# Attention weights exponentiated into transposed squares and turned by VectorE, with their sums from a column of ones, in a two-layer graph kernel

## Chip, cores and metric

One core of one Trainium2 chip. The metric is device time in microseconds of one execution; the median of three runs of the kernel before is 3092.37 us (3086.59 to 3094.2). Profiled executions have a span of their own (3078.1 us here), on which the shares of the profile are taken.

## The reference, cut to what matters

128 graphs of 64 nodes with 768 features pass two layers. Everything is float32.

```
# layer 0
p = softmax(h h^T / sqrt(768)) * adj;  attn = p / sum(p)
ctx = triu(attn,1) (h Wl^T + bl) + diag(attn) (h Ws^T + bs) + tril(attn,-1) (h Wr^T + br)
x = layernorm(h + relu(layernorm(ctx) * gamma + beta))
# layer 1, 12 heads of 64
q, k, v = x Wq + bq, x Wk + bk, x Wv + bv
scores = where(adj > 0, q k^T / 8 + beta * adj, -9e15)
out = layernorm(x + softmax(scores) v)
```

The softmax of layer 1 is what the change is about: the weighted sum of values can be divided by the sum of the exponentials afterwards.

## The kernel before, in words

The 8192 rows are walked in 16 blocks of 512 tokens (8 graphs; T = 4 tiles of 128 rows, each with two graphs). Each large product is computed by a seven-product (Strassen-Winograd) scheme, `seven()`: 7 products in the order 1, 2, 6, 5, 7, 4, 3, each in two halves j, so 14 *places* of six matmuls each. `by_tokens()` uses it for the self, left, right and value weights (128x384 a matmul), `projected()` for queries and keys (128x256), one call for each of three head groups of four heads. The two accumulators are ps_X (products 1, 6, 7, 4) and ps_Y (2, then 5 and 3), each one PSUM bank for each j. ScalarE evicts ps_X in `projected` (L522, L528) and VectorE adds it to ps_Y (L530); in `by_tokens` VectorE does both (L298 and the lines L392, L410, L501). A bank that still accumulates has to be read before its next product starts: product 7 is read while one place passes, before product 4; the other reads have three places.

A block n passes these parts in order: left (`side_part(m, "l")`, m = n + 1), right, self (`self_part`), val (`values(n)`), then `projected` three times. Layer 0 of block m and layer 1 of block n overlap, and the attention of block n - 1's last head groups is done inside the left part of block n. From the first block on, the program's order is kept as written. Two things set it: *hooks*, a table that says at which place of which part a step stands ahead of the products, and two *queues*, urgent and lazy. After each place `step()` issues one item of the queues, urgent ones first; an item marked "act" (ScalarE) or "gap" lets a lazy one follow in the same step, and no "act" item is issued after the second half of product 5 or the first half of product 7. `settle(key)` issues at once whatever is left of a key.

For a head group, `scores()` computes q k^T in 64x64 products, four in the array at a time (L548), scales and masks (L552, L567), subtracts the maximum (L568, L569), exponentiates (L570), sums (L563), divides (L564, L571). `turned_weights()` transposes the result on TensorE against an identity (L586), eight transposes for each head group, copied out of PSUM by ScalarE (L587). `weighted()` multiplies with the values (L600), and two queue items add the outcome to the residual (L606). The values of both graphs of a tile are kept so that the row half of the array matches the head's parity: `values()` evicts each result in four pieces of 64 rows (L501). `finish()` normalises and stores.

PSUM: two banks each for ps_X and ps_Y, two for transposes (ps_tr, tag tr), two for everything else (ps_mm). Weights stream from DRAM on SyncE's queue through four buffers (L293, L516); `loads()` fetches x for the residual (L728) there too, at places 0 to 3 of the self part; `squares()` loads a block in 32x32 squares on ScalarE's queue (L202), for layer 1 from place 9 of the right part, and `turned()` transposes the squares on VectorE (L211) in the self part from place 3.

Of the kernel before, what the change touches and what calls it, by code (L numbers as in the profile page):

```python
# [11 lines left out]
F32 = mybir.dt.float32  # L12
AF = mybir.ActivationFunctionType
# [31 lines left out]
def gnn_two_layers(ctx: ExitStack, tc, x, adj, wl, bl, ws, bs, wr, br, gamma, beta,  # L45
# [11 lines left out]
    wst = ctx.enter_context(tc.tile_pool(name="wst", bufs=4))  # L57
    st = ctx.enter_context(tc.tile_pool(name="st", bufs=2))
    ps_st = ctx.enter_context(tc.tile_pool(name="ps_st", bufs=2, space=PSUM))
    ps_tr = ctx.enter_context(tc.tile_pool(name="ps_tr", bufs=2, space=PSUM))  # L60
    ps_mm = ctx.enter_context(tc.tile_pool(name="ps_mm", bufs=2, space=PSUM))

    x_t = x.rearrange("b l d -> (b l) d").rearrange("(n t p) d -> n t p d", t=T, p=P)
    x_b = x.rearrange("b l d -> (b l) d").rearrange("(n k) d -> n k d", k=NTOK)
# [46 lines left out]
    def act(f):  # L111
        return f, "act"
# [17 lines left out]
    def settle(key):  # L130

        for queue in (urgent, lazy):
            while any(item[0] == key for item in queue):
                queue.popleft()[1]()


# [50 lines left out]
    def transposed(src, xT, t):  # L187

        for c0 in range(0, KC, 3):
            ps = ps_tr.tile([P, 4, P], F32, tag="tr", name="ps_x")  # L190
            for c in range(3):
                nc.tensor.transpose(ps[:, c, :], src[:, c0 + c :: KC], ident)
            nc.scalar.copy(xT[:, c0 : c0 + 3, t * P : (t + 1) * P], ps[:, 0:3, :])
# [179 lines left out]
    def sides(n):  # L373

        blk = blocks[n]
        settle(("a", n))
        aps = ps_tr.tile([P, T, P], F32, tag="tr", name="ps_a")
        for t in range(T):
            nc.tensor.transpose(aps[:, t, :], blk["a2"][:, t].rearrange("p c m -> p (c m)"), ident)  # L379
        aT = l0.tile([P, T, P], F32, tag="aT", name=f"aT_{n}")  # L380
        nc.vector.tensor_tensor(aT, aps, side.rearrange("p g l -> p (g l)")[:, None, :].to_broadcast([P, T, P]),
                                ALU.mult)
        blk["aT"] = aT
# [99 lines left out]

        return one, two

    def values(n, hooks={}):


        blk = blocks[n]
        v = l1_p.tile([P, T, 2, HP, HD], F32, tag="v", name=f"v_{n}")  # L490
        blk["v"] = v

        def last(t, h, ps, part):
            def pairs(a):
                return a.rearrange("p (j r d) -> p r j d", r=2, d=HD)

            add = pairs(bias["v"][:, h * HALF : (h + 1) * HALF] if part is None else part)
            for r in range(2):
                for g in range(2):
                    rows = slice(g * L, (g + 1) * L)  # L500
                    nc.vector.tensor_tensor(v[r * L : (r + 1) * L, t, g, h * 3 : (h + 1) * 3, :],  # L501
                                            pairs(ps)[rows, r], add[rows, r], ALU.add)

        by_tokens("v", blk["S"], last, None, hooks)

    def projected(n, hg, hooks={}):

# [24 lines left out]
        seven(HTOK, factors, first, last, hooks, True)  # L532
        blk["qk"] = qk

    def scores(n, hg, pool=None):

        blk = blocks[n]
        q, k = blk["qk"]

        s = (pool or l1s_p).tile([P, T, 2, 2, L], F32, tag="lr" if pool else "s", name="s")  # L540
        sc = [ps_mm.tile([P, T, 2, L], F32, tag="mm", name=f"sc{r}") for r in range(2)]
        for t in range(T):
            for c in range(2):
                for r in range(2):
                    rows = slice(r * HD, (r + 1) * HD)
                    for g in range(2):
                        tok = slice(t * P + g * L, t * P + (g + 1) * L)
                        nc.tensor.matmul(sc[r][g * L : (g + 1) * L, t, c, :], lhsT=q[rows, c, tok],  # L548
                                         rhs=k[rows, c, tok], start=True, stop=True)
        m8, add = blk["m8"], blk["add"]  # L550
        for r in range(2):
            nc.vector.tensor_tensor(s[:, :, :, r, :], sc[r], m8[:, :, None, :].to_broadcast([P, T, 2, L]), ALU.mult)  # L552
        s4 = s.rearrange("p t c r m -> p t (c r) m")
        s8 = s.rearrange("p t c r m -> p (t c r) m")
        mx = st.tile([P, T * 4], F32, tag="mx1", name="mx1")
        z = st.tile([P, T * 4], F32, tag="z1", name="z1")
        rz = st.tile([P, T * 4], F32, tag="rz1", name="rz1")

        def per_row(v):
            return v[:, :, None].to_broadcast([P, T * 4, L])  # L560

        def sums():
            nc.vector.tensor_reduce(z, s8, AX.X, ALU.add)  # L563
            nc.vector.reciprocal(rz, z)  # L564

        later(("s", n, hg),
              lambda: nc.vector.tensor_tensor(s4, s4, add[:, :, None, :].to_broadcast([P, T, 4, L]), ALU.add),  # L567
              lambda: nc.vector.tensor_reduce(mx, s8, AX.X, ALU.max),  # L568
              lambda: nc.vector.tensor_tensor(s8, s8, per_row(mx), ALU.subtract),  # L569
              act(lambda: nc.scalar.activation(s8, s8, AF.Exp)), GAP, sums,  # L570
              lambda: nc.vector.tensor_tensor(s8, s8, per_row(rz), ALU.mult), queue=urgent)  # L571
        blk[hg] = s

    def turned_weights(n, hg, tiles=range(T), pool=None):

        blk = blocks[n]
        settle(("s", n, hg))
        e = blk[hg]
        if 0 in tiles:
            blk["eT", hg] = (pool or l1_p).tile([P, T, 2, P], F32, tag="lr" if pool else "eT", name="eT")  # L580
        eT = blk["eT", hg]
        for t0 in tiles[::2]:
            ps = ps_tr.tile([P, 4, P], F32, tag="tr", name="ps_e")
            for t in range(2):
                for c in range(2):
                    nc.tensor.transpose(ps[:, 2 * t + c, :], e[:, t0 + t, c].rearrange("p r m -> p (r m)"), ident)  # L586
            nc.scalar.copy(eT[:, t0 : t0 + 2].rearrange("p t c i -> p (t c) i"), ps)  # L587

    def weighted(n, hg, tiles=range(T)):

        blk = blocks[n]
        xt, v, eT = blk["x"], blk["v"], blk["eT", hg]
        y = [ps_mm.tile([P, T, 2, HD], F32, tag="mm", name=f"ps_y{r}") for r in range(2)]
        for t in tiles:
            for c in range(2):
                for r in range(2):
                    rows = slice(r * L, (r + 1) * L)
                    for g in range(2):
                        cols = slice(g * L, (g + 1) * L)
                        nc.tensor.matmul(y[r][cols, t, c, :], lhsT=eT[rows, t, c, cols],  # L600
                                         rhs=v[rows, t, g, hg + c * HC, :], start=True, stop=True)

        def added(t):
            res = xt[t].rearrange("p (c k r d) -> p r c k d", c=2, k=HC, r=2)
            for r in range(2):
                nc.vector.tensor_add(res[:, r, :, hg, :], res[:, r, :, hg, :], y[r][:, t])  # L606

        def both(ts):
            for t in ts:
                added(t)  # L610

        later(("y", n, hg), *[partial(both, tiles[i : i + 2]) for i in range(0, len(tiles), 2)], queue=urgent)

    def finish(n, tiles=range(T)):
        xt = blocks[n]["x"]
# [60 lines left out]
    blocks[0]["S"] = combined(blocks[0]["xT"])  # L676
    start.close()
    l1_p = ctx.enter_context(tc.tile_pool(name="l1", bufs=1))
    l1s_p = ctx.enter_context(tc.tile_pool(name="l1s", bufs=2))

# [3 lines left out]
    for n in range(NBLK):  # L686
# [12 lines left out]
        last = n == NBLK - 1  # L699
        if p >= 0:  # L700
            one, two, three = (left, left, right) if not last else (qk[0], qk[1], qk[1])
            at(one, 1 if not last else 2, scores, p, 2)
            at(one, 1 if not last else 2, turned_weights, p, 1)
            at(one, 5, weighted, p, 1)
            at(two, 11 if not last else 2, turned_weights, p, 2)
            at(two, 13 if not last else 5, weighted, p, 2)
            at(three, 0 if not last else 6, finish, p)

        if not last:
            if n > 0:  # L710
# [6 lines left out]
                    settle(("o", n))  # L717
                    blocks[n]["sq1"], sq1["fs"] = squares(blocks[n]["x_d"])

                at(right, 9, begin1)  # L720
                fetch = {}

                def begin2():
                    fetch["fs"] = loads(m)

                at(own, 0, begin2)
                for t in range(T):
                    at(own, t, lambda t=t: fetch["fs"][t]())  # L728
                for a in range(P // Q):
                    at(right, 9 + a, lambda a=a: sq1["fs"][a]())  # L730
                at(own, 0, settle, ("f", p))

                def turn1():
# [43 lines left out]
        at(qk[1], 2, scores, n, 0)  # L777
        at(qk[2], 2, scores, n, 1)
        if not last:
            at(qk[2], 2, turned_weights, n, 0)  # L780
            at(qk[2], 5, weighted, n, 0)
        for hg in range(NHG):
            projected(n, hg, qk[hg])
    n = NBLK - 1
    values(n, {2: [partial(scores, n, 2, l0t)]})

    for t0 in (0, 2):
        for hg in range(NHG):
            turned_weights(n, hg, range(t0, t0 + 2), l0t if hg else None)
        for hg in range(NHG):  # L790
            weighted(n, hg, range(t0, t0 + 2))
            settle(("y", n, hg))
        finish(n, range(t0, t0 + 2))
        settle(("f", n))


# [29 lines left out]
```

## Time and profile before

| | before |
|---|---|
| median of runs | 3092.37 us |
| span of the profile | 3078.1 us |
| TensorE clock granted | 0.992 |
| TensorE busy / VectorE / ScalarE / GpSimd | 97% / 72% / 13% / 12% |
| TensorE busy from 200 to 2800 us | 2550.7 of 2600 us |
| one block in the middle | about 188 us |
| DMA moved | 541.2 MB, 176 GB/s over the span |

A row of groups gives the line, engine and operation, output and inputs with their shapes and count, then busy time in us and mean ns of one instruction, then the idle time of that engine before these instructions and what ended it. Matmuls are pipelined: the mean of one includes time in which the one before still runs, so the busy time, not count times mean, is what the group takes of the engine. A row of waits names who waited for whom, the total in us, how often, and the longest.

### The profile page before, as it was taken

The numbers are of one execution on the slowest core, as the hardware profiler recorded it, in microseconds if no ns is written. First come the engines' busy times: TensorE is split into PE (matmuls) and PEld (weight loads), VectorE is DVE, ScalarE is ACT, GpSimd is POOL, SyncE is SP. The second block draws the span as 40 slices with busy tenths as digits, with TensorE's granted clock in tenths as the row PEclk, the third lists the DMA queues.
The fourth block names the chain that finished last, engine by engine and source line by source line (L and its number), as shares of the span: only waits on it lengthen the run. The fifth ranks groups of instructions, "written<-read, shape, count | busy, mean of one in ns | idle before, by whom it ended". The sixth has DMA issues, their size and how long they took to land.

```text
span 3078.1 us, 45049 instructions
## 1 busy us (share of the span) xinstructions
PE 2983.9 (97%) x18144; PEld 2015.0 (65%) x18144; DVE 2227.8 (72%) x4163; ACT 396.8 (13%) x691; POOL 354.3 (12%) x317
## 2 busy tenths in 40 slices
PE   8899999999999999999999999999999999999997
PEld 5457657576675766758567585665757667575685
DVE  5758767686776867768687686867768677686756
ACT  0101102021020200202011020110201102020031
POOL 2321010110101101011010111101011010110000
PEclk9999999999999999999999999999999999999998
DMA  8663655737557474574645756456573655746433
GB/s 284 211 230 121 190 174 166 216 118 217 152 161 213 124 229 139 161 215 145 212 139 162 211 160 208 132 179 191 161 221 119 215 156 162 220 127 220 128 123 119
DMA packets 261070, 541.20 MB, mean 176 GB/s; under 512 B 28576, under 2 KB 165408, under 8 KB 260864
## 3 DMA queue, kind: packets, MB, share of 16 engines
q1 hardware_dynamic: 185424, 429.38, 44.1%
q10 hardware_dynamic: 60848, 44.05, 7.2%
q0 software_dynamic: 14592, 64.89, 5.4%
q8 instruction: 145, 2.38, 0.3%
q14 instruction: 61, 0.50, 0.0%
HBM read 473.37 MB, written 64.88 MB: 175 GB/s over the span
## 4 chain that ended last, share of the span: by engine, by line
PE 77%; DVE 7%; issue 7%; DMA 7%; POOL 1%; ACT 0%; ACTq 0%; SPq 0%; POOLq 0%; DVEq 0%
PE ps_X L269 38%; PE ps_Y L269 30%; DMA ws<-in_L_gnn_W_self_dram 6%; DVE v L501 4%; PE ps_ctx L425 3%; DVE hT L211 2%; PE sc L548 1%; PE ps_y L600 1%; PE u L331 1%; PE ps_e L586 1%; DVE u L298 1%; DMA b_l<-in_L_gnn_W_left_dram 1%; DVE stats L239 0%; PE ps_a L379 0%; DMA d_v<-t_v 0%
## 5 line engine op out<-in xcount | busy, mean ns | idle before, releaser
L269 PE MATMUL ps_X<-xT,wqk 128*128 128x256 f32 x1728 | 388.8, 379 | 0.0
L269 PEld LDWEIGHTS ps_X<-xT,wqk 128*128 128x128 f32 x1728 | 328.2, 190 | 48.1 <-issue 0.4
L269 PE MATMUL ps_Y<-S,wqk 128*128 128x256 f32 x1152 | 264.3, 379 | 0.0
L410 DVE TENSOR_TENSOR lr<-ps_Y,u 64x384 f32<-64x384 f32 x384 | 213.2, 555 | 62.6 <-PE ps_Y L269 56.2
L522 ACT ACTIVATE uqk<-ps_X,bq 128x256 f32<-128x256 f32 x144 | 68.2, 474 | 1419.5 <-PE ps_X L269 1419.5
L269 PEld LDWEIGHTS ps_Y<-S,wqk 128*128 128x128 f32 x1152 | 218.9, 190 | 29.8
L269 PE MATMUL ps_X<-wv,xT 128*128 128x384 f32 x576 | 199.2, 492 | 0.3
L239 DVE BATCH_NORM_STATS2 stats<-o 128x6 f32<-128x384 f32 x384 | 192.4, 542 | 1.8
L269 PE MATMUL ps_X<-ws,hT 128*128 128x384 f32 x540 | 181.7, 491 | 7.4 <-DMA ws<-d_s 7.4
L269 PE MATMUL ps_X<-wl,hT 128*128 128x384 f32 x540 | 183.7, 486 | 0.0
L269 PE MATMUL ps_X<-wr,hT 128*128 128x384 f32 x540 | 179.1, 486 | 0.0
L501 DVE TENSOR_TENSOR v<-ps_Y,u 64x192 f32<-64x192 f32 x384 | 136.4, 355 | 41.7 <-PE ps_Y L269 35.6
L269 PE MATMUL ps_Y<-xT,wqk 128*128 128x256 f32 x576 | 138.7, 386 | 27.8 <-DVE v L501 17.9
L269 PEld LDWEIGHTS ps_X<-wv,xT 128*128 128x128 f32 x576 | 106.7, 190 | 85.8 <-issue 9.6
L269 PEld LDWEIGHTS ps_X<-ws,hT 128*128 128x128 f32 x540 | 103.5, 192 | 79.8 <-issue 9.7
L269 PEld LDWEIGHTS ps_X<-wr,hT 128*128 128x128 f32 x540 | 102.5, 190 | 71.3
L269 PEld LDWEIGHTS ps_X<-wl,hT 128*128 128x128 f32 x540 | 100.4, 190 | 61.1
L269 PE MATMUL ps_X<-S,wqk 128*128 128x256 f32 x576 | 138.2, 385 | 0.0
L269 PEld LDWEIGHTS ps_Y<-xT,wqk 128*128 128x128 f32 x576 | 104.3, 190 | 51.6 <-issue 23.8
L298 DVE TENSOR_TENSOR u<-ps_X,bv 128x384 f32<-128x384 f32 x96 | 53.5, 557 | 114.7 <-PE ps_X L269 114.1
L298 DVE TENSOR_TENSOR u<-ps_X,bl 128x384 f32<-128x384 f32 x96 | 53.4, 556 | 112.5 <-PE ps_X L269 110.6
L619 POOL DMA_DIRECT2D out_dram<-o x64 | 34.6, 541 | 862.2 <-DVE o L618 862.0
(183 smaller groups left out, 4715.2 us busy)
## 6 DMA issues: line engine op xcount, KB each, us to landing
wqk<-qk_d SPq DMA_DIRECT2D x336, 384.0 KB, 3.0
wv<-d_v SPq DMA_DIRECT2D x64, 576.0 KB, 4.8
ws<-d_s SPq DMA_DIRECT2D x60, 576.0 KB, 9.0
wl<-d_l SPq DMA_DIRECT2D x60, 576.0 KB, 5.0
wr<-d_r SPq DMA_DIRECT2D x60, 576.0 KB, 3.7
wv<-in_L_gnn_Wv_dram SPq DMA_DIRECT2D x48, 576.0 KB, 4.0
ws<-in_L_gnn_W_self_dram SPq DMA_DIRECT2D x45, 576.0 KB, 7.4
wl<-in_L_gnn_W_left_dram SPq DMA_DIRECT2D x45, 576.0 KB, 4.1
```

The costliest lines, as they stand in the source:

```text
L211: nc.vector.transpose(xT[:, c, :].rearrange("p (s j) -> p s j", j=Q), sq[:, :, c::KC])
L239: nc.vector.bn_stats(stats[:, h, :], tiles[t][:, h * HALF : (h + 1) * HALF])
L269: nc.tensor.matmul(ps, lhsT=a, rhs=b, start=(c == 0 and i in (1, 2, 5)), stop=(c == len(fs) - 1), skip_group_check=True)
L298: nc.vector.tensor_tensor(u, ps, bias[nm][:, b * HALF : (b + 1) * HALF], ALU.add)
L331: nc.tensor.matmul(u[g * L : (g + 1) * L, t, :], lhsT=xT[:, c, tok], rhs=xT[:, c, tok], start=(c == 0), stop=(c == KC - 1))
L410: nc.vector.tensor_tensor(lr[t][half * L : (half + 1) * L, g, cols], ps[rows], bias[nm][rows, cols] if part is None else part[rows], ALU.add)
L425: nc.tensor.matmul(ps[g * L : (g + 1) * L, 0:HALF], lhsT=blk["aT"][:, t, g * L : (g + 1) * L], rhs=blk["lr"][t][:, g, cols], start=True, s ...
L501: nc.vector.tensor_tensor(v[r * L : (r + 1) * L, t, g, h * 3 : (h + 1) * 3, :], pairs(ps)[rows, r], add[rows, r], ALU.add)
L522: nc.scalar.activation(u, ps, AF.Identity, bias=bias["qk"[j]][:, c : c + 1])
L548: nc.tensor.matmul(sc[r][g * L : (g + 1) * L, t, c, :], lhsT=q[rows, c, tok], rhs=k[rows, c, tok], start=True, stop=True)
L586: nc.tensor.transpose(ps[:, 2 * t + c, :], e[:, t0 + t, c].rearrange("p r m -> p (r m)"), ident)
L619: nc.gpsimd.dma_start(out=out_t[n, t], in_=xt[t])
```

## The change

The weights are no longer summed, divided and transposed by TensorE. The exponentials are written in 32x32 squares to where each square of the transpose stands (16 instructions of 32 partitions by 256 columns for a head group, issued in four groups, or two in the left part and for the last head group), and VectorE turns the squares in place (two transposes of 128x512). The values get a 65th column of ones for each head, so that the product with the weights has the sum of exponentials beside the 64 outputs; `added()` takes its reciprocal and multiplies and adds in one instruction for each tile and head. Values are evicted whole (one piece), and three ScalarE copies, queued after the value part, swap the halves that belong to the other rows; the last block evicts in place as before. The pool for transposes is gone and its two banks go to ps_mm (four). In `scores()`, any unfinished exponentials are settled first, as there is one score buffer instead of two, with two buffers for the transposed weights. The layer-1 squares are loaded from place 10 of the left part, and x from place 8 of the right part. In the left part the last head group's weighted sums stay ahead of place 13; its two turns are issued after places 11 and 12.

The diff, cut to its core:

```diff
-    ps_tr = ctx.enter_context(tc.tile_pool(name="ps_tr", bufs=2, space=PSUM))
-    ps_mm = ctx.enter_context(tc.tile_pool(name="ps_mm", bufs=2, space=PSUM))
+    ps_mm = ctx.enter_context(tc.tile_pool(name="ps_mm", bufs=4, space=PSUM))
...
+            if not in_place:
+                nc.vector.tensor_tensor(v[:, t, :, heads, 0:HD], pairs(ps), add, ALU.add)
+                return
...
+        if not in_place:
+            low, high = v[0:L, :, 1, :, 0:HD], v[L:P, :, 0, :, 0:HD]
+            swap = l0t.tile([P, T, HP, HD], F32, tag="lr", name="swap")
+            later(("v", n), act(lambda: nc.scalar.copy(swap[0:L], high)), act(lambda: nc.scalar.copy(high, low)),
+                  act(lambda: nc.scalar.copy(low, swap[0:L])), queue=urgent)
...
+        settle("e")
+        settle(("m", n))
...
-        def sums():
-            nc.vector.tensor_reduce(z, s8, AX.X, ALU.add)
-            nc.vector.reciprocal(rz, z)
...
+            for a in groups:
+                rows = slice(a * Q, (a + 1) * Q)
+                for b in range(P // Q):
+                    cols = slice(b * Q, (b + 1) * Q)
+                    nc.scalar.activation(e[cols, :, rows], pairs[rows, :, cols], AF.Exp)
+
+        def turn(h):
+            e = blk["eT", hg][:, h * 2 : h * 2 + 2].rearrange("p t c i -> p (t c i)")
+            nc.vector.transpose(e, e)
...
-              act(lambda: nc.scalar.activation(s8, s8, AF.Exp)), GAP, sums,
-              lambda: nc.vector.tensor_tensor(s8, s8, per_row(rz), ALU.mult), queue=urgent)
+              *[act(partial(exponentials, range(a, a + at_once))) for a in range(0, P // Q, at_once)], GAP,
+              partial(turn, 0), partial(turn, 1), queue=urgent)
...
-        for t0 in tiles[::2]:
-            ps = ps_tr.tile([P, 4, P], F32, tag="tr", name="ps_e")
-            for t in range(2):
-                for c in range(2):
-                    nc.tensor.transpose(ps[:, 2 * t + c, :], e[:, t0 + t, c].rearrange("p r m -> p (r m)"), ident)
-            nc.scalar.copy(eT[:, t0 : t0 + 2].rearrange("p t c i -> p (t c) i"), ps)
...
+        def added(h, r):
+            ps = y[r, h]
+            rz = st.tile([P, 2, 2], F32, tag="rz1", name="rz1")
+            nc.vector.reciprocal(rz, ps[:, :, :, HD])
...
+                    nc.vector.scalar_tensor_tensor(res[:, r, c, hg, :], ps[:, t, c, 0:HD], rz[:, t, c : c + 1],
+                                                   res[:, r, c, hg, :], ALU.mult, ALU.add)
+
+
+        urgent.extendleft(reversed([(("y", n, hg), partial(added, h, r)) for h in halves for r in range(2)]))
...
-    l1s_p = ctx.enter_context(tc.tile_pool(name="l1s", bufs=2))
+    l1s_p = ctx.enter_context(tc.tile_pool(name="l1s", bufs=1))
+    l1e_p = ctx.enter_context(tc.tile_pool(name="l1e", bufs=2))
+
+    v = l1_p.tile([P, T, 2, HP, HD + 1], F32, tag="v", name="v")
+    nc.gpsimd.memset(v[:, :, :, :, HD], 1.0)
...
-            at(one, 1 if not last else 2, turned_weights, p, 1)
...
-            at(two, 11 if not last else 2, turned_weights, p, 2)
             at(two, 13 if not last else 5, weighted, p, 2)
...
-                at(right, 9, begin1)
+                at(left, 10, begin1)
...
-                at(own, 0, begin2)
+                at(right, 8, begin2)
```

## The prediction

> **What bounds the kernel now.** I read the page's busy table first, then the slices, the groups by line, TensorE's waits, and a timeline of one block.
>
> ```profile
> PE 2983.9 (97%) x18144; PEld 2015.0 (65%) x18144; DVE 2227.8 (72%) x4163; ACT 396.8 (13%) x691; POOL 354.3 (12%) x317
> ```
>
> The groups by line (busy us, mean ns of one, idle before):
>
> ```profile
> L269 PE MATMUL ps_X<-xT,wqk 128*128 128x256 f32 x1728 | 388.8, 379 | 0.0
> ...
> L501 DVE TENSOR_TENSOR v<-ps_Y,u 64x192 f32<-64x192 f32 x384 | 136.4, 355 | 41.7 <-PE ps_Y L269 35.6
> ...
> L586 PE MATMUL ps_e<-ident,s 128*128 128x128 f32 x384 | 53.1, 282 | 2.5 <-ACT eT L587 2.5
> ```
>
> TensorE is busy 97% of 3078.1 us at a granted clock of 0.992, and its matmuls carry the chain that ended last. So the change is worth what it takes from TensorE's own work and from its waits, less the waits it adds; VectorE (72%) and ScalarE (13%) have room on average, but in-order queues can be late in one place. The question is then where the 94 us lie in which TensorE is idle. Its waits (total, times, longest):
>
> ```profile
> PE ps_Y L269 <- DMA ws<-in_L_gnn_W_self_dram: 21.3, 13, 3.8
> PE ps_Y L269 <- DVE v L501: 17.9, 14, 1.3
> PE ps_Y L269 <- PE ps_X L269: 9.8, 14, 0.7
> ...
> PE ps_a L379 <- ACT eT L587: 4.1, 14, 0.3
> ```
>
> From 200 to 2800 us the stretches show 2550.7 us of TensorE in 2600: 49.3 idle. These four rows hold about all of it (one 3.8 us piece of the first lies earlier). The second and third are one event: the timeline shows the third ending 0.1 us after a value eviction (L501) does, so both are the first products of the query/key projection waiting for a PSUM bank whose values VectorE writes out in four pieces each. The first row is the self weights, late in each block while activations, squares and outputs are being moved (DMA share above 1 from 1320 to 1340 us).
>
> **What the Trainium skill says.** "ScalarE: Activation LUTs", section What ACT_TABLE_LOAD costs: an ACTIVATE with immediate scale and bias takes 186 ns + 0.833 ns an element, whatever the function. For 256 elements 399 ns; this trace has 417 (L350, 128x256), and I use 417. "VectorE: DVE Perf Modes", The three transpose paths: VectorE's transpose turns 32x32 blocks only, which is why the exponentials are written square by square; the trace shows L211 on such squares, 1091 ns for 128x512. "TensorE: Matmul & The Clock Gate", Step-by-step: what each phase is for: matmuls stay in program order, only weight loads are pulled ahead. So a matmul that waits holds all products behind it; no trace line here contradicts it.
>
> **The change part by part.**
>
> *Transposes.* 384 transposes of the weights leave TensorE: 53.1 us (L586). All lie on the path, so −53.1. The waits of the transpose behind ScalarE's copies (ps_a, 14 times 0.3) go with them: −4.1.
>
> *Exponentials.* 48 of 128x1024 (1057 ns) become 768 of 32x256. None of 32 partitions is in the trace; bounds: 417 ns (L350, same length) as the upper, about 310 if consecutive ones overlap as the skill's page says. I take 417: 16 x 0.417 = 6.7 us a head group, on ScalarE, which also evicts the projections. ScalarE's total: 396.8 − 50.7 − 51.3 (copies L587) + 768 x 0.417 + swaps 64 = 679 us, 22%. Queued behind a group of four exponentials (1.7 us) are the evictions of ps_X (474 ns), for which VectorE's add and TensorE's next product into that bank wait. A place of the projection is 1.3 us of TensorE (5.34 us for four). The tight bank is the seventh product's: it must be read within one place. The queue keeps exponentials out of the two places before it. In the block at 1420 the scores are ready (L569) at 1425.8; two groups then end at 1429.2, and the eviction there starts at 1429.25 and is due by 1430.4. The other evictions have three places, 4 us. So nothing on the path, with about 0.7 us to spare.
>
> *Turns.* 96 transposes of 128x512 on VectorE, 1.08 us each: 104 us. They replace the sums, their reciprocals and the scaling (58.3 + 12.1 + 58.5). Values whole: 512 pieces of 355 ns (181.9 us) become 120 of 557 and 32 of 355 (78 us). The weighted sums: 384 adds (82.5) become 768 of 64 columns and 192 reciprocals; between 162 ns (L360, 128x4) and 279 (L606, 128x128) I take 200: 154 + 35 us. VectorE: −393 + 371, about 2206 us (2175 to 2270). Its total hides under TensorE.
>
> *Values.* With one 0.56 us eviction instead of 1.46 us of four, VectorE has no backlog when the projection begins: −17.9 − 9.8 = −27.7. The three half-swaps are 15 x 3 copies of 64x1536, by the slope between 128x384 (478) and 128x512 (585) 1.43 us each, at the front of the first projection. They end some 30 us before the values are used (third projection), and delay evictions with four places of room: no cost.
>
> *Loads moved.* The squares go from the right part to the left part, x from the self part to the right part, so the two 1.5 MB sets no longer meet in the stretch with DMA share above 1. The stretches at the end of the left part have 0.3 to 0.5. The self weights then land in time: −17.5 (21.3 without the early piece of 3.8).
>
> *Ones column.* 3072 products of 65 columns for 64: 58.5/64 = +0.9.
>
> *The wait it adds.* In the left part the last head group's two turns are issued after places 11 and 12, and its weighted sums stand ahead of place 13. The timeline of one block, before:
>
> ```profile
> 1483.58 2.10 PE L269 MATMUL ps_X<-wl,hT 128*128 128x384 f32 x6
> ...
> 1485.52 2.10 PE L269 MATMUL ps_Y<-wl,S 128*128 128x384 f32 x6
> ...
> 1485.72 1.12 DVE L410 TENSOR_TENSOR lr<-ps_X,bl 64x384 f32<-64x384 f32 x2 [0.74 <-PE ps_X L269]
> 1487.55 1.16 PE L600 MATMUL ps_y<-v,eT 64*64 64x64 f32 x64
> 1487.65 1.12 DVE L410 TENSOR_TENSOR lr<-ps_Y,u 64x384 f32<-64x384 f32 x2 [0.81 <-PE ps_Y L269]
> 1488.64 2.20 PE L269 MATMUL ps_Y<-wl,S 128*128 128x384 f32 x6
> ```
>
> Put the turns in: eviction of place 11 to 1486.84, first turn to 1487.93; eviction of place 12 to 1489.05, second turn to 1490.14. The first half of the weighted products (0.55 us) can start at 1488.0, the second at 1490.2, and place 13 at 1490.75 instead of 1488.64: 2.1 us. Behind the waiting matmul is all of the right part, so it is on the path: 14 blocks x 2.1 = +29.4 (1.0 to 2.5 each: 14 to 35). The other two weighted sums have four or more places between turn and use.
>
> *Tail.* Before, 27.9 us pass from the last product (3050.20) to the end. After it VectorE has a turn more to do (1.1), six weighted sums of 2 reciprocals and 8 products (2.0 us instead of about 1.7 with the waits), but the last transposes and copies (2.2 us of wait) are gone and two head groups fit in the banks. I get 24.4 + 6.4 us of output DMA, about +3.
>
> Sum: −53.1 − 4.1 − 27.7 − 17.5 + 0.9 + 29.4 + 3 = −69. From 3092.4: **3023 us**.
>
> **Rivals.**
> 1. *The turns are no wait* (VectorE runs ahead, or the first half's products cover it): −98, 2994 us. For it: VectorE is idle 0.7 to 0.8 us before both evictions shown. Against: 2.2 us of work per 1.94 us place cannot be done before its inputs exist.
> 2. *ScalarE and the DMA take half back.* The loads now meet outputs and right weights, and the wait moves rather than goes (+17.5); an exponential of 0.55 us makes the two groups 4.4 us and the bank of the seventh product some 0.4 us late in 15 projections (+6); the turns cost the high 2.5 us each (+6): 3053 us. For it: only 0.7 us spare there, and x and outputs are still 3 MB together. Against: landing times of 3.7 to 5 us outside the crowded stretch, where a piece is issued some 12 us ahead.
> 3. *ScalarE becomes the bound of the projections*: small exponentials of 0.8 us would make 12.8 us for a head group against 5.2 us of products in its four places, leaving some 3 us uncovered after the evictions' slack in 2 projections of 15 blocks: +90 on my sum, 3113 us, slower. For it: 32-partition shapes are not in the trace, and the count rises from 48 to 768. Against: the price per element and the 128x256 row agree.
>
> **How the numbers follow.** My case 0.62, the first rival 0.13, the second 0.19, the third 0.06. The likeliest gives 3023. The low bounds of the turns (14 us) and a tail of 0 give 3005, the first rival 2994, the second 3053; the range takes in all of these, 2993 to 3054. Outside it are the third rival and the far sides of the first two, together under 2 in 10. Faster by over 0.3% (below 3083) holds in all but the third and odd cases: 0.92; same 0.02; slower 0.06.
>
> **What would show it.** No L586 or L587 groups; the waits on L501 and on the self weights gone from TensorE's list; instead a wait of ps_y on VectorE's transpose, 14 times, 1.5 to 2 us, in the left part. Exponentials near 417 ns, turns near 1.08 us, y products near 200. TensorE busy near 2932 us. It would be wrong if TensorE shows new waits on ScalarE's uqk, if a wait on wr or ws weights comes back, or if y products take over 300 ns.

## The result, and the profile after

The changed kernel takes 2997.33 us (2995.84 to 2998.13, four runs) against 3089.48 us of the kernel before measured beside it (3083.96 to 3094.2, four runs): a ratio of 0.9702 [0.9683, 0.9721], or −92 us. The prediction was 3023 us, −69 us; its range (2993 to 3054) holds the result, near its lower end. In the profiles the span goes from 3078.1 to 2995.2 us, −82.9, at the same granted clock of 0.992. The two measures differ because the profiled execution of the kernel before took 3079.84 us, less than any of the four runs measured beside the change (median 3089.48), while that of the changed kernel lies near its median (2996.95).

The page's busy table of the changed kernel (busy us, share of the span, instructions):

```profile
PE 2924.5 (98%) x17760; PEld 1980.5 (66%) x17760; DVE 2156.5 (72%) x4331; ACT 677.7 (23%) x1360; POOL 355.2 (12%) x318
```

TensorE's busy time fell from 2983.9 to 2924.5 us (−59.4), and its idle time, span less busy, from 94.2 to 70.7 (−23.5). ScalarE has 1.7 times the work and is still at 23%.

The groups by line of the changed kernel (busy us, mean ns of one, idle before):

```profile
L577 ACT ACTIVATE eT<-s 32x256 f32<-32x256 f32 x768 | 317.8, 414 | 149.8 <-DVE s L586 139.7
...
L615 DVE SCALAR_TENSOR_TENSOR o<-ps_y,rz,o 128x64 f32<-128x64 f32 x768 | 165.0, 277 | 6.8
...
L581 DVE STREAM_TRANSPOSE eT<-eT 128x512 f32<-128x512 f32 x96 | 65.9, 700 | 36.8 <-ACT eT L577 36.1
L605 PE MATMUL ps_y<-v,eT 64*64 64x65 f32 x3072 | 64.3, 226 | 26.7 <-DVE eT L581 17.1 <-DVE rz L611 6.5 <-DVE v L503 0.8
...
L498 DVE TENSOR_TENSOR v<-ps_Y,u 128x384 f32<-128x384 f32 x90 | 50.2, 558 | 54.8 <-PE ps_Y L268 53.8
```

No group of transposes of the weights is left on TensorE. An exponential takes 414 ns, a turn 700 ns, a whole value eviction 558 ns. What TensorE waits for (total us, times, longest):

```profile
PE ps_y L605 <- DVE eT L581: 17.1, 14, 1.2
...
PE ps_y L605 <- DVE rz L611: 6.5, 5, 4.1
...
PE ps_X L268 <- ACT uqk L529: 3.4, 1, 3.4
```

The rows of 17.9 and 9.8 (values) and 4.1 us (ps_a) are gone, and of the 21.3 us on the self weights one wait of 0.8 us is left. One row is new in almost every block: the weighted products behind the turn, 14 times, 1.22 us each. The longest wait on rz lies in the tail. The bank that ScalarE empties (uqk) is waited for once, in block 14 of 0 to 15. There a square root, with a table load of 1.28 us before and after it, stands on ScalarE's queue between two groups of exponentials, and the eviction stands behind all of it:

```profile
2835.80 1.28 ACT L246 ACT_TABLE_LOAD   x1
2837.09 0.20 ACT L246 ACTIVATE std<-std 128x4 f32<-128x4 f32 x1
2837.31 1.28 ACT L577 ACT_TABLE_LOAD   x1
2838.61 1.69 ACT L577 ACTIVATE eT<-s 32x256 f32<-32x256 f32 x4
2840.32 0.47 ACT L529 ACTIVATE uqk<-ps_X,bq 128x256 f32<-128x256 f32 x1
```

The place of the new wait behind the turn, in a timeline of one block:

```profile
1252.20 2.10 PE L268 MATMUL ps_Y<-wl,S 128*128 128x384 f32 x6
1252.40 1.12 DVE L409 TENSOR_TENSOR lr<-ps_X,bl 64x384 f32<-64x384 f32 x2
1253.56 0.71 DVE L581 STREAM_TRANSPOSE eT<-eT 128x512 f32<-128x512 f32 x1
1254.34 1.12 DVE L409 TENSOR_TENSOR lr<-ps_Y,u 64x384 f32<-64x384 f32 x2
1254.42 0.70 PE L605 MATMUL ps_y<-v,eT 64*64 64x65 f32 x32
1255.47 0.71 DVE L581 STREAM_TRANSPOSE eT<-eT 128x512 f32<-128x512 f32 x1
1256.33 0.70 PE L605 MATMUL ps_y<-v,eT 64*64 64x65 f32 x32 [1.22 <-DVE eT L581]
1256.96 2.20 PE L268 MATMUL ps_Y<-wl,S 128*128 128x384 f32 x6
```

It goes as the prediction drew it: turn after the eviction of place 11, turn after that of place 12, half of the weighted products after each, and place 13 behind them. Only the turns are shorter.

Mean lengths of the parts of a block, between the starts of their first products, over 13 blocks of each timeline (us):

| kernel | block | left | right | self | val | three projections |
|---|---|---|---|---|---|---|
| before | 188.23 | 33.61 | 27.09 | 28.95 | 33.88 | 64.70 |
| after | 182.26 | 33.03 | 27.09 | 27.09 | 33.64 | 61.40 |

13 blocks of 5.97 us are 77.6 of the 82.9 us. The rest is a shorter start (−7.1 us until the first left part), a last stretch of large products (from the last left part on) 1.2 us longer, and a tail, from the last large product to the end, of 30.2 us for 27.9.

### The profile page after: what moved, and what is told of

Read it like the earlier page. It is cut to its first block, busy times and chain, and to the rows that moved or that the text cites. A ratio compares the mean times of both kernels' runs of the same rounds, so it can differ in the third digit from the quotient of the medians.

```text
span 2995.2 us, 45114 instructions
## 1 busy us (share of the span) xinstructions
PE 2924.5 (98%) x17760; PEld 1980.5 (66%) x17760; DVE 2156.5 (72%) x4331; ACT 677.7 (23%) x1360; POOL 355.2 (12%) x318
## 3 DMA queue, kind: packets, MB, share of 16 engines
q1 hardware_dynamic: 185424, 429.38, 46.7%
## 4 chain that ended last, share of the span: by engine, by line
PE 88%; issue 7%; DMA 2%; DVE 1%; POOL 1%; ACTq 0%; POOLq 0%; SPq 0%; DVEq 0%
PE ps_X L268 46%; PE ps_Y L268 34%; PE ps_ctx L424 3%; PE sc L559 2%; PE u L330 1%; PE ps_y L605 1%; DVE lr L409 1%; DMA b_l<-in_L_gnn_W_left_dram 1%; DMA wl<-d_l 0%; DMA bs<-in_L_gnn_b_self_dram 0%; DVE eT L581 0%; DMA d_v<-t_v 0%; DMA ws<-d_s 0%; PE ps_a L378 0%; PE ps_x L191 0%
## 5 line engine op out<-in xcount | busy, mean ns | idle before, releaser
L577 ACT ACTIVATE eT<-s 32x256 f32<-32x256 f32 x768 | 317.8, 414 | 149.8 <-DVE s L586 139.7
L615 DVE SCALAR_TENSOR_TENSOR o<-ps_y,rz,o 128x64 f32<-128x64 f32 x768 | 165.0, 277 | 6.8
L537 DVE TENSOR_TENSOR q<-ps_Y,uqk 128x256 f32<-128x256 f32 x144 | 60.2, 418 | 112.4 <-ACT uqk L529 60.2
L268 PE MATMUL ps_Y<-wv,S 128*128 128x384 f32 x384 | 133.2, 490 | 0.0
```

The source lines that it names most:

```text
L268: nc.tensor.matmul(ps, lhsT=a, rhs=b, start=(c == 0 and i in (1, 2, 5)), stop=(c == len(fs) - 1), skip_group_check=True)
L537: nc.vector.tensor_tensor(dst, ps, part, ALU.add)
L577: nc.scalar.activation(e[cols, :, rows], pairs[rows, :, cols], AF.Exp)
L615: nc.vector.scalar_tensor_tensor(res[:, r, c, hg, :], ps[:, t, c, 0:HD], rz[:, t, c : c + 1], res[:, r, c, hg, :], ALU.mult, ALU.add)
```

## The experiments

The theory: TensorE sets the end throughout. The change takes its transposes and three waits away (values, self weights, ps_a) and adds one, behind the turns. ScalarE stays hidden because its exponentials come in groups of four between the evictions. The rivals: the turns cost nothing; the gain lies elsewhere than in the loads or the values; ScalarE's total is what matters and not its order. A ratio is to the kernel before, run beside; a difference to the changed kernel is to its median under again, in part from another chip (the kernel before takes 3087 to 3090 us on the three chips). "Idle" is span less TensorE's busy time in the profile.

**The changed kernel again** (label again): no edit.

> The changed kernel once more, as the yardstick of this chip. Both theories: 2997 us within 3, ratio to before 0.968 to 0.972.

Measured: 2996.26 us, ratio 0.9698 [0.9679, 0.9717], span 2994.7. The result repeats within 1.1 us.

**The last weighted sums one place later** (late_weighted):

```diff
-            at(two, 13 if not last else 5, weighted, p, 2)
+            at(right if not last else two, 0 if not last else 5, weighted, p, 2)
```

> The last head group's weighted sums moved from ahead of place 13 of the left part to ahead of place 0 of the right part, one place (1.94 us) later; nothing else. Theory (the second turn is on TensorE's path): the trace has 1.22 us of wait and some 0.3 us of late start in 14 blocks, so 17 to 23 us fewer than the changed kernel, about 2977 us, and no wait of ps_y on VectorE's transpose. Rival (the wait stands in for other lateness of VectorE, which then shows at the next bank): the wait reappears under another name and the time stays within 3 us of the changed kernel.

Measured: 2975.12 us, ratio 0.9628 [0.9606, 0.9649], span 2967.9. Its busy table, and the first rows of TensorE's waits:

```profile
PE 2917.8 (98%) x17760; PEld 1978.6 (67%) x17760; DVE 2154.2 (73%) x4331; ACT 677.1 (23%) x1360; POOL 354.7 (12%) x318
```

```profile
PE ps_X L268 <- DMA ws<-d_s: 6.8, 1, 6.8
PE ps_y L605 <- DVE rz L611: 6.6, 5, 4.1
```

The wait on the turn is gone, and with it 21.1 us of the runs (27.3 of the span: 20.6 idle and 6.7 busy). So the turns did cost time, which the first rival denied, and this version is faster than both kernels. The profiled execution is the shortest of the four (spans of 2967.9 to 2976.4 us, at granted clocks of 0.994 to 0.990), and the changed kernel had two stretches of lowered clock near its end that this one lacks. So the 21.1 us are the better figure: the 13 blocks in the middle, where neither kernel has a lowered clock, give 21.3 us, 17.4 idle and 3.9 busy, or 1.64 us a block. The left part shrinks from 33.03 to 31.29 us, while the right part, which now carries the products, grows by 0.10. From 200 to 1400 us the stretches show TensorE busy for 1200.00 of 1200 us.

**The loads put back** (loads_back): the changed kernel with squares and x loaded where the kernel before has them.

```diff
-                at(left, 10, begin1)
+                at(right, 9, begin1)
...
-                at(right, 8, begin2)
+                at(own, 0, begin2)
...
-                    at(right, 8 + t, lambda t=t: fetch["fs"][t]())
+                    at(own, t, lambda t=t: fetch["fs"][t]())
...
-                    at(left, 10 + a, lambda a=a: sq1["fs"][a]())
+                    at(right, 9 + a, lambda a=a: sq1["fs"][a]())
```

> The changed kernel with the layer-1 squares loaded in the right part and x in the self part again. Theory (the two sets of loads met): the wait on the self weights comes back, 17 to 25 us slower than the changed kernel, about 3017 us, and the runs scatter by several us as before's do (3084 to 3094), since the scatter comes from that wait. Rival (the wait went because the rest of the schedule moved): within 3 us of the changed kernel, runs within 3 us of each other.

Measured: 3038.53 us, ratio 0.9837 [0.9813, 0.9862], span 3037.3: 42 us slower than the changed kernel, about twice what was expected. The four runs lie within 6.1 us, those of the changed kernel within 3.5. The top row of TensorE's waits, then two rows of VectorE's:

```profile
PE ps_X L268 <- DVE u L297: 28.5, 26, 2.4
```

```profile
DVE xT L210 <- DMA sq<-x1d: 61.1, 9, 7.4
...
DVE xT L210 <- DMA ws<-in_L_gnn_W_self_dram: 38.2, 5, 8.2
```

Here TensorE does not wait for the weights themselves, as in the kernel before, but for VectorE's eviction of u. And VectorE waits up to 8.2 us ahead of a turn of squares. One such place in the timeline:

```profile
1319.49 1.08 DVE L210 STREAM_TRANSPOSE xT<-sq 128x512 f32<-128x512 f32 x1 [8.17 <-DMA ws<-in_L_gnn_W_self_dram]
1320.49 0.52 DVE L297 TENSOR_TENSOR u<-ps_X,bs 128x384 f32<-128x384 f32 x1
...
1321.07 9.59 PE L268 MATMUL ps_X<-ws,hT 128*128 128x384 f32 x24 [2.36 <-DVE u L297]
```

The turn stands at the head of VectorE's queue until its data is there, the eviction behind it starts at 1320.49, and TensorE's next product waits 2.36 us for the bank. The second wait row names the self weights, but a turn reads only squares, so what holds it must be the squares (up to 20.3 us from issue to landing here, up to 15.5 in the kernel before). The products after the wait are slow as well: 24 take 9.59 us, where 24 undisturbed ones take some 7.9 (12 take 4.03). The granted clock from 1320 to 1325 is 0.66. Over the run, idle grows by 27.3 us and busy by 14.8, together the 42.1 us of the span. The self part goes from 27.09 to 30.02 us, the other parts stay. The theory was right about the part and the sign; it had not counted the busy time, and in this kernel the way from late data to TensorE leads through VectorE's queue.

**The loads moved alone** (before_loads): the same four edits, the other way, in the kernel before.

> The kernel before with the loads moved alone. Theory (parts add up): the wait on the self weights goes, 17 to 25 us fewer than before, ratio about 0.993, and the runs scatter less. Rival (the loads only land in time because the left part is otherwise changed): less than 5 us.

Measured: 3051.78 us, ratio 0.9883 [0.9858, 0.9908], span 3048.8. That is −36.4 us in the runs and −29.3 in the span: idle −17.2, which is the predicted 17.5, and busy −12.1. The waits on values stay at 17.9 and 9.8 us. The runs now lie within 2.7 us, where those of the kernel before lie within 18.4 on the same chip (3076.6 to 3094.97). So much of the scatter of the kernel before came with these loads; not all scatter does, as late_weighted, with the loads moved, lies within 7.7 us. That the profile before, taken on a short execution, understates their cost fits, but no longer execution was profiled. In the changed kernel the same loads cost 42 us: their price depends on what stands around them.

Not all of the 29.3 us lies in the regular blocks. In the 13 middle ones the difference is 24.2 us, 17.1 idle and 7.1 busy, with two stretches of lowered clock in the kernel before. Of the other busy time, 4.2 us lie ahead of the first left part, where the kernel before has two more such stretches, one of them behind its early wait of 3.8 us.

**Values evicted in pieces again** (pieces): the changed kernel with the old four evictions, without the swaps.

```diff
-            values(n, val)
+            values(n, val, True)
```

> The changed kernel with the values of every block evicted in four pieces where they belong (as the last block does it), and no swap on ScalarE. Theory (the first projection's two products waited for VectorE's backlog from the pieces): two waits of 1.3 and 0.7 us in 15 blocks come back, 26 to 32 us slower than the changed kernel, about 3026 us. Rival (the lighter VectorE load elsewhere removed the backlog): less than 8 us.

Measured: 3035.73 us, ratio 0.9825 [0.9806, 0.9844], span 3032.6: +39.5 us, more than expected. TensorE's waits:

```profile
PE ps_Y L268 <- DVE v L503: 18.0, 14, 1.3
...
PE ps_Y L268 <- PE ps_X L268: 9.9, 14, 0.7
```

Both rows come back as they were, so whole values are what removed them, not the new queue or the freed banks. Again the rows are not the whole cost: idle +26.8, busy +10.6 (in the 13 middle blocks, with no lowered clock in either kernel, +25.9 and +9.3). The difference lies in the projections, 61.40 to 63.87 us a block.

**Exponentials in pairs of groups** (pairs_of_groups): eight rather than four in a row on ScalarE's queue, the same count and total.

```diff
-    def scores(n, hg, at_once=1, pool=None):
+    def scores(n, hg, at_once=2, pool=None):
...
-            at(one, 1 if not last else 2, scores, p, 2, 1 if last else 2)
+            at(one, 1 if not last else 2, scores, p, 2, 2)
```

> The changed kernel with the exponentials issued in two groups of eight instead of four groups of four in the projections too; the same instructions in all. Theory (the bank of the seventh product has 0.7 us to spare, so grouping is what keeps ScalarE off the path): in the second projection two groups of 3.4 us end some 2.8 us after the seventh product's eviction is due, in the third the last eviction is some 1 us late, so waits of TensorE on ScalarE of 3 to 5 us in 15 blocks: 45 to 75 us slower than the changed kernel. Rival (ScalarE at 23% has room whatever the order): within 5 us of the changed kernel.

Measured: 3132.65 us, ratio 1.0144 [1.0112, 1.0176], span 3132.2: slower than the kernel before, and 136 us above the changed kernel, where 45 to 75 were expected. ScalarE's busy time is 675.5 us, as before the edit. TensorE's waits:

```profile
PE ps_X L268 <- ACT uqk L529: 44.6, 15, 6.8
PE sc L559 <- DVE k L537: 27.8, 14, 2.0
```

and one place in the timeline, with the same place of the next block:

```profile
1623.09 6.80 ACT L577 ACTIVATE eT<-s 32x256 f32<-32x256 f32 x16
1629.91 0.47 ACT L529 ACTIVATE uqk<-ps_X,bq 128x256 f32<-128x256 f32 x1
...
1630.44 5.49 PE L268 MATMUL ps_X<-xT,wqk 128*128 128x256 f32 x12 [2.70 <-ACT uqk L529]
...
1822.41 2.86 PE L268 MATMUL ps_X<-xT,wqk 128*128 128x256 f32 x12 [2.70 <-ACT uqk L529]
```

Sixteen exponentials run back to back, and the eviction of the tight bank stands behind them. ScalarE holds TensorE up, as the third rival had it, but through the order on the queue and not through its total, which is the same. The two products have the same wait of 2.70 us, yet 12 matmuls take 5.49 us in one and 2.86 in the other. The stretches of 5 us after them (stretch, length, busy us and count of TensorE, weight loads, VectorE, ScalarE, GpSimd, granted clock, DMA share, GB/s) tell why:

```profile
1630.00:1635.00 5.00, 4.56 (x11) 3.67 (x12) 3.94 (x8) 1.22 (x3) 0.00 (x0) 0.50 0.05 17
...
1825.00:1830.00 5.00, 5.00 (x25) 4.41 (x24) 4.67 (x14) 0.95 (x2) 0.00 (x0) 1.00 0.43 134
```

The granted clock is 0.50 in the one and 1.00 in the other. Of the 14 waits of 2.70 us, seven are followed by 2.86 us for 12 matmuls and seven by 4.35 to 5.49. Idle grows by 90.3 us and busy by 46.7. The lower clock is in the busy part.

The second row (k) is the same cause one part later. In the third projection eight exponentials stand ahead of the eviction of the keys, and the first scores of the left part wait for it:

```profile
1660.21 3.38 ACT L577 ACTIVATE eT<-s 32x256 f32<-32x256 f32 x8
1663.62 0.47 ACT L535 ACTIVATE k<-ps_X,bk 128x256 f32<-128x256 f32 x1
1664.70 1.04 PE L559 MATMUL sc<-k,q 64*64 64x64 f32 x56 [1.99 <-DVE k L537]
```

The expectation had this at about 1 us and no lowered clock. Of the 9.15 us by which a block is longer, 4.68 lie in the projections and 4.46 in the left part.

**A turn that reads neighbouring columns** (flat_turn): the 168 turns of squares in the two layers read 512 columns in a row instead of every sixth. The turned squares then hold other features, so this kernel computes something else, with as many instructions of the same shape.

```diff
-            nc.vector.transpose(xT[:, c, :].rearrange("p (s j) -> p s j", j=Q), sq[:, :, c::KC])
+            nc.vector.transpose(xT[:, c, :], sq.rearrange("p s f -> p (s f)")[:, c * NTOK : (c + 1) * NTOK])
```

> The transposes of the loaded squares (not of the exponentials) read 512 neighbouring columns instead of every sixth; they then turn the wrong columns, so the data of both layers is permuted and only the time is read. Theory (the 700 ns of the new turns against 1080 are due to the step between columns read): these 168 transposes fall from 1080 to about 700 ns and VectorE loses about 64 us of busy time, the whole stays within 0.3% as VectorE is not the bound there. Rival (in-place output or the place in the schedule makes the difference): they stay at 1080 ns.

Its group of turns for layer 0:

```profile
L210 DVE STREAM_TRANSPOSE hT<-sq 128x512 f32<-128x512 f32 x84 | 58.9, 702 | 0.0
```

702 ns instead of 1084: the step between the columns read is what makes the turn of squares dearer than the turn of exponentials. The time stays (2999.18 us, one run), although VectorE's busy time falls by 61 us: on average VectorE hides.

**Idle transposes put back** (idle_transposes): eight transposes of the identity ahead of each head group's scores, in the changed kernel, into a bank that nobody reads. They stand for the removed ones, without a wait on data or a copy; they are at another place and of other data, and that they cost the same is assumed.

```diff
+        idle_ps = ps_mm.tile([P, 4, P], F32, tag="mm", name="idle_ps")
+        for c in range(8):
+            nc.tensor.transpose(idle_ps[:, c % 4, :], ident, ident)
```

> The changed kernel with eight transposes of the identity against itself ahead of each head group's scores, whose result nobody reads: the same 384 transposes on TensorE that the change took away, without copies or waits. Theory (the busy time of L586, 53.1 us, counts the end of one that still runs while the next product does; the timeline shows 0.93 to 0.97 us for eight): 43 to 48 us slower than the changed kernel, about 3042 us. Rival (the busy time is what they take): 53 us or more, 3050 us.

Measured: 3039.48 us, ratio 0.9846 [0.9831, 0.986], span 3037.0: +43.2 us in the runs, +41.8 in the span. The rival of 53 us falls. The new group by line:

```profile
L554 PE MATMUL idle_ps<-ident 128*128 128x128 f32 x384 | 49.8, 273 | 0.0
```

Even here the group's busy time (49.8) is above what the group adds to the span (41.8; 34.1 in the 13 middle blocks, 0.87 us for eight transposes). So the busy time of a group is not, as was said ahead of the prediction, what it takes of the engine. That the ends of these records overlap the products behind them explains it, but is argued.

**The output of the block settled earlier near the end** (late_settled): late_weighted, and in the block before the last, the next block's layer norm forced out ahead of the first scores. This was to remove the wait on uqk.

```diff
+        if n == NBLK - 2:
+            at(qk[1], 2, settle, ("o", m))
```

> The weighted sums one place later, as before, and in addition the last block's layer-0 normalisation settled ahead of the scores of block 14's first head group, so that no square root and no table load stands between two groups of exponentials there. Theory (that square root holds ScalarE in the seventh product's tight place, 3.4 us of wait and 1.8 us of slower products after it, once): 4 to 6 us fewer than with the sums alone moved, about 2969 us, and no wait on uqk. Rival (the burst of VectorE work that it brings costs as much): no difference within 3 us.

Measured: 2973.08 us, ratio 0.9629 [0.9613, 0.9646], span 2970.2: no difference from late_weighted (0.9628). The wait falls from 3.4 to 2.2 us and stays. These two are the fastest versions found, and the runs do not tell them apart.

## Why the prediction was right or wrong

Each isolated part has an idle and a busy effect on TensorE. The signs are those of the change; each pair is the difference of two profiles. The last two columns are the 13 middle blocks alone, without start, end and tail.

| part | from | predicted | idle | busy | sum | idle, 13 blocks | busy, 13 blocks |
|---|---|---|---|---|---|---|---|
| transposes | idle_transposes to after | −53.1 | −1.4 | −40.4 | −41.8 | 0.0 | −34.1 |
| values | pieces to after | −27.7 | −26.8 | −10.6 | −37.4 | −25.9 | −9.3 |
| loads | before to before_loads | −17.5 | −17.2 | −12.1 | −29.3 | −17.1 | −7.1 |
| turn wait | late_weighted to after | +29.4 | +20.6 | +6.7 | +27.3 | +17.4 | +3.9 |
| sum of four | | −68.9 | −24.8 | −56.4 | −81.2 | −25.6 | −46.6 |
| after − before | | −69 | −23.5 | −59.4 | −82.9 | −29.4 | −48.2 |

In the middle blocks the idle time that the four parts leave over is 3.8 us, and the ps_a wait that went is 13 times 0.3; of the busy time 1.6 us is left over. Over the whole span the four come within 2 us of the change, but start and end hold stretches of lowered clock that differ from execution to execution. The sum takes the loads' price in the kernel before; with their price in the changed kernel (−42.1) it would be 13 us too much. By the runs the parts are −43, −39, −36 and +21, together −97 against the measured −92.

*Transposes: mechanism right, size off.* The step took the group's busy time (53.1 us) as what leaves the path; the runs show 42 to 43 for as many. The Trainium skill, "Perfetto Trace Analysis", Identifying the Most-Contended Engine, says that TensorE's matmul busy share is no good measure of how near it is to its limit, because pipelined instructions look smaller in the trace. Here the busy time of a group errs the other way: the group costs 0.8 of it.

*Values and loads: idle right within 1 us, busy time left out.* The prediction equated a wait with its row. 17.5 and 27.7 us are indeed what the idle time changed by, but busy time went as well, 12.1 and 10.6 us, of which 7.1 and 9.3 lie in the middle blocks. This is the main term that was mis-sized: together 22.7 us of busy time, of which the 11 us too many for the transposes hide half. In the runs, the loads give 7 us more again. That is most of the distance between −82.9 and −92.

*The turn wait: found in place, count and kind.* 14 times in the left part, as forecast. Taken at 2.1 us each (29.4), it is 1.22 us of idle in the row, and 1.64 us a block or 21 us in all by experiment. The turn was priced at the squares' 1.08 us and takes 0.70, because the columns that it reads are neighbours (flat_turn). With 0.71 us for a turn the prediction's own sum gives an estimate of 1.4 us: the second eviction ends at 1488.77, the turn at 1489.48, the products at 1490.03 instead of 1488.64. Measured are 1.34 us of idle time a block, and 0.30 of busy time that the sum did not have.

*Exponentials: right.* 414 ns for the 417 taken, ScalarE 677.7 us for 679. The price in the Trainium skill, "ScalarE: Activation LUTs", What ACT_TABLE_LOAD costs, gives an estimate of 399 for 256 elements. The overlap of consecutive instructions that the same section states, and the lower bound of 310 that rests on it, did not show: 16 in a row took 6.80 us, 425 ns each. The spare time of the tight bank, put at 0.7 us, is about 0.6 in the one place followed, the second projection of a middle block (eviction done at 1381.75, next product due about 1382.35). It gave way once, in block 14, behind the square root and its table loads, which the prediction had not counted on ScalarE's queue there.

*VectorE: total under the range.* 2156.5 us for 2206 (2175 to 2270). The turns account for 38 us of it (66 instead of 104). The multiply-and-add instructions on the products' outcome ("y products" in the prediction) take 165 us in all for 154; their mean of 277 ns includes overlap (four in the tail take 0.86 us). The swaps take 1.47 us for 1.43 and nobody waits for them.

*Tail.* +2.3 us for +3. The start (−7.1 us) was not in the prediction.

*Rivals.* The first (2994 us) is nearer to the result than the forecast, and still wrong: the wait of 14 turns is there, and removing it gives 21 us. The second's waits of loads did not move elsewhere, and the bank was late once instead of 15 times. The third did not occur: an exponential takes 414 ns, not 800. That ScalarE can hold the projections up at an unchanged total is what pairs_of_groups shows.

*Luck in the number.* The transposes and the turns were over-priced by some 10 and 8 us, in opposite directions, and the waits on values and loads under-priced by some 12 and 19 (by the runs). The forecast came out 23 us short of the gain, and only its range, which reaches to the first rival, holds the result; that these errors in part cancel was luck.

## What to carry to other kernels

A wait of TensorE cost more than its row here: in the middle blocks some 0.3 to 0.4 us of busy time each time, more where the clock fell behind it. A group's busy time overstates what removing it gives when its instructions are pipelined, here by a fifth to a quarter. So a forecast of −69 can hold errors of opposite sign; test each term by itself, and compare stretches of the trace in which the granted clock is the same. When work is moved to a hidden engine, its total matters less than how many of its instructions stand in a row ahead of the one that somebody waits for: the same 768 exponentials were hidden in fours and cost 136 us in eights.

## What the runs showed of the hardware that was not expected

*Some 2 us of idle time within one stretch of 3.41 us halve the clock.* In pairs_of_groups identical waits of 2.70 us are followed in half of the cases by microseconds at a granted clock of 0.50, which cost 1.5 to 2.6 us each. In all eleven traces the granted clock is 1.00 or 0.50, nothing between. Ahead of the tail, every stretch at 0.50 lasts 3.41 us or two or three times that, and those of one trace begin whole multiples of 3.413 us apart, to 0.01 us. On this grid the two equal waits shown above lie differently (columns as above):

```profile
1626.40:1629.81 3.41, 1.33 (x7) 0.83 (x5) 0.00 (x0) 3.32 (x9) 0.00 (x0) 1.00 0.56 185
1629.81:1633.23 3.42, 2.79 (x7) 2.26 (x8) 2.81 (x6) 0.92 (x3) 0.00 (x0) 0.50 0.12 43
...
1817.55:1820.96 3.41, 2.16 (x10) 1.55 (x9) 0.33 (x1) 3.32 (x9) 0.00 (x0) 1.00 0.50 131
1820.96:1824.37 3.41, 1.96 (x9) 1.76 (x10) 1.99 (x5) 2.01 (x6) 0.00 (x0) 1.00 0.31 100
1824.37:1827.79 3.42, 3.42 (x18) 3.01 (x17) 3.15 (x7) 0.65 (x2) 0.00 (x0) 1.00 0.35 120
```

The first leaves TensorE idle for 2.08 us of one stretch of the grid, and the next one has half the clock. The second is split into 1.25 and 1.45 us, and the clock stays. From the first left part to the last large product the traces hold 9078 grid stretches at full clock. All 22 with 2.0 us or more of idle time are followed by one at half clock, of the 21 with 1.8 to 2.0 us 15, and of the 9035 with less one. Two short waits in one stretch count together: 0.76 and 1.19 us ahead of 543.93 in pairs_of_groups were followed by half clock from 544.37. The Trainium skill, "TensorE: Matmul & The Clock Gate", Part 1: The HAM clock gate, says that the clock is halved after an idle window of about 3.4 us, and that this window runs freely. The halving and the free-running window agree with these traces; but a window did not have to be idle throughout, about 1.8 to 2.0 of its 3.41 us were enough.

*A wait costs without a lower clock too.* In pieces, the 26 waits of the 13 middle blocks, none over 1.3 us, bring 9.3 us of busy time, 0.36 us each; the 13 waits on the turn bring 3.9, 0.30 each. In these blocks neither kernel has a lowered clock. Matmuls that follow one another overlap at their ends, and a wait breaks this. That this is the cause is argued; the number is measured.

*A transpose on VectorE depends on the step of its input.* 128x512 float32 takes 0.70 us from neighbouring columns and 1.08 from every sixth.
